# A new opening for a four-direction scan layer: order of the first loads, fillers and weight products on TensorE, earlier requests for the second step

## The chip, the cores and the metric

The kernel runs on one core of a Trainium2 chip. The metric is the device time of one execution in microseconds (us); runs of one kernel are summarised by their median. The core has TensorE (PE, matrix products into PSUM, the accumulator memory of eight banks), VectorE (DVE), ScalarE (ACT), GpSimd (POOL), SyncE (SP, which issues nearly all transfers here) and 16 DMA engines. Each engine works through its own instructions in order and waits for others on semaphores.

## What is computed

The input `x` is 4 images of 128 channels and 96x96 points, float32. Each is normalised over 32 groups of four channels, read along four directions (rows, rows reversed, columns, columns reversed), put through the same scan layer, and the four results are fused by a 1x1 product and added to `x`. Cut to what matters:

```python
def _scan1d(x, ...):                               # x: sequences of 9216 points
    t = _grouped1x1(x, in_proj_w, in_proj_b, G)    # 4 groups of 32 channels
    u, gate = (t[:, :HID], t[:, HID:])
    u = jax.nn.silu(u)
    u = lax.conv_general_dilated(u, dw_w, ...)     # depthwise, 5 taps
    s = _conv1x1(u, ssm_in_w)
    a = DMIN + (DMAX - DMIN) * jax.nn.sigmoid(_conv1x1(u, ssm_delta_w, ssm_delta_b))
    bb = jnp.tanh(_conv1x1(u, ssm_b_w, ssm_b_b))
    cc = jnp.tanh(_conv1x1(u, ssm_c_w, ssm_c_b))
    prefix = jnp.cumsum(jnp.log(a), axis=-1)
    hst = jnp.exp(prefix) * jnp.cumsum(bb * s * jnp.exp(-prefix), axis=-1)
    u = u + _conv1x1(cc * hst + ssm_d[None, :, None] * s, ssm_out_w)
    u = _grouped1x1(u * jax.nn.sigmoid(gate), mix_w, mix_b, G)
    return _conv1x1(u, out_proj_w, out_proj_b)

def _gn(v, G=32, eps=1e-5):                        # mean and variance of a group
    ...
x = x + fuse(_scan1d of the four readings of _gn(x))
```

## The kernel before

**Tiling.** A sequence is cut into `NS` = 6 steps (lines of 16 x 96 points), a step into `R` = 4 phases (every fourth point), so that a tile has `N` = 384 points. Two directions run side by side (`s` = 0, 1) in one phase of the outer loop, which has 8: two orders (columns "V", rows "H") for each of 4 images. One turn of the main loop, `pair(t)`, handles two units (both `s`) of one step and phase; there are 192 turns. The second half of each phase's steps reads the mirrored data that the first half wrote to DRAM (`kept_sil`, `kept`).

**A turn.** It convolves (`conv`, `conv_less` on TensorE for half of the channels, `taps` on ScalarE and VectorE for the other half, with the first tap, `first_tap`, on ScalarE and the following ones as `scalar_tensor_tensor` on VectorE, L667), multiplies by the four scan weights (`proj`), scans (`recurrence`), and, six turns later, makes gates and outputs (`gates_and_out`, `gating`) and accumulates them into `acc` (`accumulate`). `front(t + R)` is work for one step ahead: it multiplies `x_in` by the normalised weights (`in_proj`, 4 banks of PSUM), applies silu on ScalarE (`silu`, L511), asks for the next step's rows (`after_front`, L269) and for the store of finished silus (`keep_silu`, L491). The instructions are kept in the order written (`manual_schedule`), on every engine and on SP's queue, from `start()` on; what stands ahead of it is ordered by the scheduler.

**The statistics.** For the first image x is loaded into `acc` in eight transfers (`load_x`, L296) and VectorE makes `bn_stats` of 24 pieces as they land (L298). `stats_finish` then goes through `bn_aggr` (L188), a product with `gmean` that averages over groups (`pm`), some tiny VectorE work, a second product (`pv`), `std` by the Sqrt table on ScalarE (L211), the table of silu (L213), the scaled weights `wn` (L230) and a last group of products (`pb`) for the biases `bn`. Each averaging product is done by `product` as four products of 32 columns each (L134, the helper `mm`). For the other three images the same function is run in pieces, one in every turn with phase 2 or 3 (`stats_piece`), with the biases in two turns: the first has `gm4` times `wn` and a copy and spread on VectorE (L249, L250), the second the product with `id32` (L254). It takes the PSUM bank in `free[0]`.

**The opening.** Weights come in three transfers: `small` (42 KB), `fuse` (512 KB) and `main` (384 KB), all issued by ScalarE (L291), beside x on SP. TensorE folds the output weights: 8 products L380, copied by ScalarE to `w_of`, 8 products L387 scaled into `w_fin`, 12 products of one column for the bias `b_fin` (L395). `stay_busy` issues products that nobody reads (L302): four with 512 columns ahead of the statistics' products, one with 256 and one with 512 between them. `start()` then does step 0: four `burst(0, g)` of 8 products each, their silus, then for each g `burst(1, g)`, silus and `after_front(0, g)`. So the second step's rows are asked for by

```python
for s in range(2):
    load_front(step + 1, s, slice(64 * s + 32, 64 * s + 64), slice(g, g + 1))
if g == R - 1:
    for s in range(2):
        load_front(step + 1, s, slice(64 * s, 64 * s + 32), slice(0, R))
```

and the silus of step 0 are stored one or two at a time by the first turns, `keep_silu((1, 2, 1, 0)[t] if t < R else 0)`. Inside the first `proj`, `front(R, ...)` stands between the products of the two halves of `u`; turn 0 calls `first_tap(2)` ahead of it.

Of the kernel before, what the change touches and what calls it, by code (L numbers as in the profile page):

```python
# [67 lines left out]
def conv_preact_kernel(  # L68
# [60 lines left out]
    def bank(i):  # L129
        return psum[:, i, :]  # L130
# [45 lines left out]
    def product(o, lhsT, rhs):  # L176
        for c in range(4):
            mm(o, c, lhsT[:, 32 * c : 32 * c + 32], rhs, True, True)

    def stats_finish(b):  # L180
# [10 lines left out]
        product(pm[:, 0:1], gmean, mv[:, 0:1])  # L191
# [10 lines left out]
        for e in range(2):  # L202
            product(pv[:, e : e + 1], gmeans[:, e, :], ex)
# [8 lines left out]

# [26 lines left out]
        product(pb[:, 0:4], wn, gm4)  # L239
        if b == b0:  # L240
            for g in range(4):
                for q in range(R):
                    mm(pb[:, 4 + g : 5 + g], q, wn[0:32, 32 * g : 32 * g + 32], mean[0:32, :], True, True)
            nc.vector.tensor_sub(bn, b_in, pb[:, 0:8])
        else:
            nc.vector.tensor_sub(bn[:, 0:4], b_in[:, 0:4], pb[:, 0:4])
            spread = sp.tile([P, 4], F32, tag="spread", name=f"spread_{b}")
            shift = sp.tile([P, 1], F32, tag="shift", name=f"shift_{b}")
            nc.vector.tensor_copy(shift, pb[:, 0:1])  # L249
            nc.vector.tensor_scalar_mul(spread, gmask, shift)  # L250
            yield
            pq = bank(free[0])
            for q in range(R):
                mm(pq[:, 0:4], q, id32, spread, True, True)  # L254
            nc.vector.tensor_sub(bn[:, 4:8], b_in[:, 4:8], pq[:, 0:4])
# [33 lines left out]
    def load(src, name, pool=wp):  # L289
        t = pool.tile(list(src.shape), F32, tag=name, name=name)  # L290
        nc.scalar.dma_start(t, src)  # L291
        return t
# [6 lines left out]

    def stay_busy(n):  # L300
        if n:
            nc.tensor.matmul(  # L302
                bank(free[0] ^ 1)[:, :n], w_fin[:, 0, 0, :],
                w_fin.rearrange("p d j c -> p (d j c)")[:, :n], start=True, stop=True,
                skip_group_check=True,
            )
# [11 lines left out]
    load_x([(6, 4)])  # L318
    w_out_fuse = load(fuse, "fuse", pp)
    load_x([(10, 4)])  # L320
    w_main = load(main, "main")
    load_x([(14, 4), (18, 4), (22, 2)])
# [76 lines left out]
    for _ in range(4):  # L399
        stay_busy(512)  # L400
# [737 lines left out]
```

## Time and profile before

| what | us |
|---|---|
| median of 3 runs | 1834.1 (1832.43 to 1839.93) |
| the profiled execution: its time | 1834.1 |
| its span | 1832.3 |
| TensorE busy in the span | 1804.5 (98%) |
| ScalarE busy | 1567.5 (86%) |
| VectorE busy | 1451.7 (79%) |
| GpSimd busy | 1423.1 (78%) |
| mean granted clock of TensorE | 0.995 |

The time is 1.8 us more than the span; the difference lies outside what the profile records. Engine rows in the views have a start, a busy time, engine, line, operation, output and inputs, and a count; a bracket tells how long the engine was idle before and what ended that. One fp32 product shows as two records on TensorE (`x8` is four products), so counts there are twice those in the code. The granted clock is a share of full speed. Busy time of TensorE hides pipelining, and it hides the clock: the same product is longer when the clock is at half.

### The profile page before, as it was taken

What the parts mean: (1) busy time and instruction counts of PE and PEld (TensorE: products, weight loads), DVE (VectorE), ACT (ScalarE), POOL (GpSimd) and SP (SyncE); (2) the same over time, 40 slices, a digit from 0 to 9 for tenths busy, and PEclk for the clock granted to TensorE, in tenths of its full rate; (3) what the DMA queues carried; (4) which work ended last, traced back from release to release, by engine and by line L of the source; (5) the groups of instructions that cost most, each with busy time, mean ns of one, the idle gap of its engine ahead of it and who ended that gap; (6) DMA issues with size and microseconds to landing.
All of it is one profiled execution on the core that took longest, in us unless ns stands there. A gap on an engine that the chain in (4) does not pass through costs nothing.

```text
span 1832.3 us, 57345 instructions
## 1 busy us (share of the span) xinstructions
PE 1804.5 (98%) x24092; PEld 651.7 (36%) x24092; DVE 1451.7 (79%) x1460; ACT 1567.5 (86%) x2762; POOL 1423.1 (78%) x1469
## 2 busy tenths in 40 slices
PE   7999999999999999999999999999999999999998
PEld 4333333333333333333333333333333333333333
DVE  5888878877878888877778888877877778777886
ACT  4888888988888888888888888888888888888974
POOL 2487887778778888787877888887877788887785
PEclk8999999999999999999999999999999999999999
DMA  6755563444965566344696547443476634635434
GB/s 196 198 192 179 163 191 111 160 144 147 301 234 180 167 193 184 104 141 140 212 299 203 170 162 208 135 159 112 160 238 222 225 127 153 193 103 179 148 122 156
DMA packets 147826, 321.18 MB, mean 175 GB/s; under 512 B 14193, under 2 KB 115697, under 8 KB 147569
## 3 DMA queue, kind: packets, MB, share of 16 engines
q1 hardware_dynamic: 147136, 316.56, 53.8%
q8 instruction: 190, 3.11, 0.7%
q10 hardware_dynamic: 432, 0.96, 0.1%
q14 instruction: 68, 0.55, 0.1%
HBM read 185.21 MB, written 132.25 MB: 173 GB/s over the span
## 4 chain that ended last, share of the span: by engine, by line
PE 95%; ACT 3%; DMA 1%; DVE 1%; issue 0%; POOL 0%; SPq 0%; ACTq 0%; DVEq 0%; POOLq 0%
PE psum L134 81%; PE psum L536 8%; PE psum L530 5%; ACT sil L511 1%; ACT psum L544 1%; DMA x_in<-in_xs 0%; PE psum L302 0%; ACT u L650 0%; DMA fuse<-in_fuse 0%; ACT t L717 0%; DVE u L616 0%; ACT t L705 0%; PE psum L380 0%; ACT psum L665 0%; ACT u L648 0%
## 5 line engine op out<-in xcount | busy, mean ns | idle before, releaser
L667 DVE SCALAR_TENSOR_TENSOR psum<-sil,small,psum 128x768 f32<-128x768 f32 x576 | 589.1, 1023 | 32.3 <-ACT psum L665 6.6
L134 PE MATMUL psum<-u,w_fin 128*32 128x384 f32 x6176 | 552.6, 488 | 0.2 <-ACT t L705 0.2
L616 DVE SCALAR_TENSOR_TENSOR u<-gate,psum 128x768 f32<-128x768 f32 x376 | 349.9, 953 | 251.1 <-ACT gate L553 113.7
L134 PE MATMUL psum<-u,main 128*32 128x384 f32 x6144 | 536.0, 489 | 0.1
L786 POOL TENSOR_TENSOR acc<-ys,acc 128x384 f32<-128x384 f32 x374 | 413.6, 1127 | 36.2 <-ACT ys L767 10.4
L740 POOL TENSOR_TENSOR t<-t,t 64x384 f32<-64x384 f32 x191 | 233.4, 1222 | 156.1 <-PE psum L530 74.9
L134 PEld LDWEIGHTS psum<-u,w_fin 128*32 128x32 f32 x6176 | 189.2, 110 | 321.5 <-issue 221.0
L134 PEld LDWEIGHTS psum<-u,main 128*32 128x32 f32 x6144 | 181.6, 110 | 327.8 <-issue 199.3
L544 ACT COPY psum<-u 128x768 f32<-128x768 f32 x352 | 276.8, 799 | 22.0 <-DVE u L667 10.3
L707 POOL TENSOR_SCALAR t<-tm 64x384 f32<-64x384 f32 x191 | 176.7, 925 | 151.5 <-ACT tm L699 101.1
L134 PE MATMUL psum<-sil,band 128*32 128x384 f32 x3072 | 285.9, 488 | 3.1 <-ACT ys L769 3.1
L741 POOL TENSOR_TENSOR t<-t,t 64x384 f32<-64x384 f32 x191 | 246.4, 1290 | 15.0
L536 PE MATMUL psum<-t,main 32*128 32x384 f32 x1536 | 242.1, 515 | 3.3 <-ACT psum L544 2.6
L665 ACT ACTIVATE psum<-sil,small 128x768 f32<-128x768 f32 x192 | 174.2, 907 | 62.3 <-DVE u L616 52.3
L553 ACT ACTIVATE gate<-psum,bnorm 128x384 f32<-128x384 f32 x384 | 192.9, 582 | 28.4 <-PE psum L530 26.4
L708 POOL TENSOR_TENSOR t<-t,tm 64x384 f32<-64x384 f32 x192 | 195.1, 1016 | 15.3
L667 DVE SCALAR_TENSOR_TENSOR u<-sil,small,psum 128x768 f32<-128x768 f32 x192 | 194.9, 1015 | 8.2 <-PE psum L134 0.5
L511 ACT ACTIVATE sil<-psum,bnorm 128x385 f32<-128x385 f32 x384 | 192.1, 585 | 3.1 <-PE psum L134 0.9
L134 PE MATMUL psum<-sil,less 64*32 64x384 f32 x3072 | 168.1, 495 | 0.0
L530 PE MATMUL psum<-x_in,wn 32*128 32x384 f32 x768 | 162.1, 528 | 3.9 <-DVE shift L249 1.4
L769 ACT COPY ys<-psum 128x384 f32<-128x384 f32 x281 | 130.1, 477 | 29.1 <-PE psum L134 28.2
L134 PEld LDWEIGHTS psum<-sil,band 128*32 128x32 f32 x3072 | 89.9, 109 | 174.7 <-issue 93.9
(98 smaller groups left out, 1500.3 us busy)
## 6 DMA issues: line engine op xcount, KB each, us to landing
sil<-sil SPq DMA_DIRECT2D x128, 770.0 KB, 6.9
kept<-gate SPq DMA_DIRECT2D x80, 768.0 KB, 3.7
gate<-kept SPq DMA_DIRECT2D x76, 768.0 KB, 4.8
x_in<-in_xs SPq DMA_DIRECT2D x192, 96.2 KB, 2.5
out<-acc SPq DMA_DIRECT2D x48, 384.0 KB, 8.2
acc<-in_xr SPq DMA_DIRECT2D x38, 384.0 KB, 6.9
xs<-in_xr SPq DMA_DIRECT2D x72, 192.0 KB, 4.7
x_in<-in_xs SPq DMA_DIRECT2D x184, 48.1 KB, 3.9
```

What stands on the lines that cost most here:

```text
L134: nc.tensor.matmul(o[r, : rhs.shape[-1]], lhsT, rhs, start=start, stop=stop, skip_group_check=True)
L511: nc.scalar.activation(sils[step][:, s, j, g, :], bank(bk)[:, : N + 1], AF.Silu, bias=bn[:, 1:2] if j else bn[:, 4 + g : 5 + g],)
L530: nc.tensor.matmul(bank(to)[:, :N], stats[un["b"]][0][r, s, :], x_in[s][r, q, off : off + N], start=True, stop=True)
L536: nc.tensor.matmul(bank(SSM + 2 * s + j)[:, :N], w_so[r, bass.ts(j, P)], z[r, :], start=bi not in seeded, stop=True, skip_group_check=True)
L544: nc.scalar.copy(psum[:, SSM + 2 * s : SSM + 2 * s + 2, :N], us[bi][:, s])
L553: nc.scalar.activation(gv[:, s, j, :], bank(to[2 * s + j])[:, :N], AF.Tanh, bias=bn[:, 2 + j : 3 + j], scale=0.5,)
L616: nc.vector.scalar_tensor_tensor(v, g, 1.0, pz, ALU.add, ALU.mult)
L667: nc.vector.scalar_tensor_tensor(us[i][:, :, 1, :] if k == K - 1 else part, src, w_tap[:, k : k + 1], part, ALU.mult, ALU.add,)
L708: nc.gpsimd.tensor_mul(ta[0:64, p, :], tb[0:64, :], tm[0:64, :])
L740: engine.tensor_mul(ta[0:64, p, :], tb[64:P, :], ta[64:P, p, :])
L741: engine.tensor_add(tb[0:64, :], ta[0:64, p, :], tb[0:64, :])
L786: adder.tensor_add(part, y, part)
```

## The change

The averaging products are no longer cut in four: `product` is gone, and each is one product of 128 columns. For the later images the biases are made in one turn, as for the first, with 16 tiny products of `mean`, and the spread with `id32` is gone. `stats_piece` in turns with `ahead` set stands behind `conv_less`. `fuse` and `main` are issued by SP, behind most of x and behind all of x. VectorE's two scalings of weights go to GpSimd, behind the making of `band` and `less`. Folding is spread: three filler products with 512 columns of x, the eight `w_out` products, and then the eight `w_mix` products in four calls of `fold`, between the products of the statistics; the 12 products of one column stand behind the fourth fold and ahead of `pb`. ScalarE copies two results at a time. `stay_busy` is gone. The second step's rows are asked for by `load_rows` between the bursts, all four silu stores of step 0 at the end of `start()`, and turn 0's `first_tap(2)` is put between the second and the third silu of `front(R)`.

```diff
-    def product(o, lhsT, rhs):
-        for c in range(4):
-            mm(o, c, lhsT[:, 32 * c : 32 * c + 32], rhs, True, True)
...
-        product(pm[:, 0:1], gmean, mv[:, 0:1])
+        nc.tensor.matmul(pm[:, 0:1], gmean, mv[:, 0:1], start=True, stop=True)
...
-            product(pv[:, e : e + 1], gmeans[:, e, :], ex)
+            nc.tensor.matmul(pv[:, e : e + 1], gmeans[:, e, :], ex, start=True, stop=True)
...
             nc.scalar.activation(std, var, AF.Sqrt)
-
+            after_std()
             nc.scalar.activation(first_table, std[:, 0:1], AF.Silu)
...
-        product(pb[:, 0:4], wn, gm4)
-        if b == b0:
-            for g in range(4):
-                for q in range(R):
-                    mm(pb[:, 4 + g : 5 + g], q, wn[0:32, 32 * g : 32 * g + 32], mean[0:32, :], True, True)
-            nc.vector.tensor_sub(bn, b_in, pb[:, 0:8])
-        else:
-            nc.vector.tensor_sub(bn[:, 0:4], b_in[:, 0:4], pb[:, 0:4])
-            spread = sp.tile([P, 4], F32, tag="spread", name=f"spread_{b}")
-            shift = sp.tile([P, 1], F32, tag="shift", name=f"shift_{b}")
-            nc.vector.tensor_copy(shift, pb[:, 0:1])
-            nc.vector.tensor_scalar_mul(spread, gmask, shift)
-            yield
-            pq = bank(free[0])
+        nc.tensor.matmul(pb[:, 0:4], wn, gm4, start=True, stop=True)
+        for g in range(4):
             for q in range(R):
-                mm(pq[:, 0:4], q, id32, spread, True, True)
-            nc.vector.tensor_sub(bn[:, 4:8], b_in[:, 4:8], pq[:, 0:4])
+                mm(pb[:, 4 + g : 5 + g], q, wn[0:32, 32 * g : 32 * g + 32], mean[0:32, :], True, True)
+        nc.vector.tensor_sub(bn, b_in, pb[:, 0:8])
...
-    load_x([(6, 4)])
-    w_out_fuse = load(fuse, "fuse", pp)
-    load_x([(10, 4)])
-    w_main = load(main, "main")
-    load_x([(14, 4), (18, 4), (22, 2)])
+    load_x([(6, 4), (10, 4), (14, 4), (18, 4)])
+    w_out_fuse = load(fuse, "fuse", pp, nc.sync)
+    load_x([(22, 2)])
+    w_main = load(main, "main", wp, nc.sync)
...
+    def fold(d):
+        pt = bank((4, 5, 0, 1)[d])[:, : 2 * P]
         for j in range(2):
             nc.tensor.matmul(
+                pt[:, bass.ts(j, P)], w_mix[:, j, :], w_of[:, d, j, :], start=True, stop=True
             )
+        nc.scalar.mul(w_fin[:, d].rearrange("p j c -> p (j c)"), pt, 0.5)
+
+    with tc.manual_schedule(engines=engines):
+        for _ in range(3):
             nc.tensor.matmul(
+                bank(7), accf[:, bass.ds(10 * SC, P)], accf[:, bass.ds(10 * SC, 512)],
+                start=True, stop=True,
             )
...
+        pieces = stats_finish(b0, lambda: fold(3))
+        next(pieces)
+        fold(0)
+        next(pieces)
+        fold(1)
+        fold(2)
+        next(pieces)
...
+        for i, (lhsT, rhs) in enumerate(terms):
+            nc.tensor.matmul(
+                pf[:, 0:1], lhsT, rhs, start=(i == 0), stop=(i == len(terms) - 1)
+            )
+        for _ in pieces:
+            pass
+        nc.vector.tensor_add(b_fin, pf[:, 0:1], b_fuse)
...
-                front(R, (5, 4, 2, 3))
+                first = front_parts(R, (5, 4, 2, 3), half=True)
+                next(first)
+                next(first)
+                first_tap(2)
+                for _ in first:
+                    pass
...
         if ahead:
             accumulate(waiting.pop(0), w[1], *final)()
             free[0] = w[0]
-            stats_piece()
             if not between:
                 conv_less(i, banks)
+            stats_piece()
...
-        keep_silu((1, 2, 1, 0)[t] if t < R else 0)
...
-        pieces = stats_finish(b0)
-        for wait in (0, 256, 512, 0, 0):
-            next(pieces, None)
-            stay_busy(wait)
...
         for g in range(R):
             burst(0, g)
+        load_rows(0, slice(0, R))
         for g in range(R):
             silus(0, g)
         new_u(0)
         for g in range(R):
             burst(1, g)
+            if g in (0, R - 1):
+                load_rows(1, slice(min(g, 1), g + 1))
             silus(1, g)
-            after_front(0, g)
+            to_keep.append((0, g))
...
         taps(0, (2, 3, 4))
+        keep_silu(R)
```

## The prediction

> **What bounds the kernel now.** I read the page's engine shares first, then its slices, then TensorE's waits, the chain of the first 80 us, and the timeline and clock of the stretches the change touches.
>
> ```profile
> PE 1804.5 (98%) x24092; PEld 651.7 (36%) x24092; DVE 1451.7 (79%) x1460; ACT 1567.5 (86%) x2762; POOL 1423.1 (78%) x1469
> ...
> PE   7999999999999999999999999999999999999998
> ```
>
> TensorE sets the time; only the first and last slices are not full. Outside the opening a saved microsecond can only be one in which TensorE waits, and its waits are few:
>
> ```profile
> PE psum L380 <- DMA fuse<-in_fuse: 6.3, 1, 6.3
> PE psum L134 <- DMA x_in<-in_xs: 4.3, 2, 2.8
> ...
> PE psum L530 <- DVE shift L249: 1.4, 3, 0.5
> ...
> PE psum L530 <- DVE bnorm L255: 1.2, 3, 0.4
> ```
>
> The two waits for `x_in` stand at 34.8 (2.83 us, second step) and 61.6 (1.42 us, third step) in the timeline. The start itself is this chain of rows:
>
> ```profile
> 10.54 8.44 DVE L298 BATCH_NORM_STATS2 bn<-acc 128x6 f32<-128x384 f32 x18
> 12.21 1.84 PE L395 MATMUL psum<-small,w_of 128*128 128x1 f32 x16
> 13.92 1.41 PE L395 MATMUL psum<-small,fuse 128*128 128x1 f32 x8
> 15.19 6.68 PE L302 MATMUL psum<-w_fin 128*128 128x512 f32 x8
> 19.01 0.80 DVE L188 BATCH_NORM_AGGREGATE mv<-bn 128x2 f32<-128x144 f32 x1
> 21.80 0.24 PE L134 MATMUL psum<-mv,gmean 128*32 128x1 f32 x8
> 23.08 1.12 PE L302 MATMUL psum<-w_fin 128*128 128x512 f32 x2
> 25.59 4.84 ACT L511 ACTIVATE sil<-psum,bnorm 128x385 f32<-128x385 f32 x10 [0.45 <-PE psum L134]
> ```
>
> `mv` is ready at 19.81, but its product runs at 21.80, behind four fillers that take 1.67 us each. The clock tells why they are slow (columns: stretch, length, PE, PEld, DVE, ACT, POOL, clock, DMA share, GB/s):
>
> ```profile
> 14.80:17.80 3.00, 3.00 (x6) 1.54 (x7) 3.00 (x7) 0.26 (x1) 0.00 (x0) 0.50 1.04 322
> 17.80:21.00 3.20, 3.20 (x5) 1.35 (x4) 1.98 (x4) 0.00 (x0) 0.00 (x0) 0.50 1.07 213
> 38.40:41.60 3.20, 3.20 (x36) 0.71 (x32) 3.09 (x4) 2.38 (x5) 0.00 (x0) 0.50 0.16 36
> ```
>
> Finer stretches put the drops at 14.4 and 38.3 and the returns at 21.2 and 41.7, all whole multiples of about 3.41 us apart. The first drop follows the one-column products of L395, the second the 2.83 us wait.
>
> **The change, part by part.** Gains have a minus.
>
> 1. *Statistics sooner.* VectorE loses 0.66 + 0.15 us of weight scaling, which GpSimd does between 10.9 (its last `band`) and its next work at 42.1, free there. It also idled 1.46 and 1.57 us for x, which shared the DMA with `fuse` and `main`. Summed over stretches of 2 us, the DMA moved 4.76 MB until 14.0 and 5.55 MB until 16.0. In the new order `small`, x and `fuse` are 5.29 MB, so the last pieces arrive at 15.3 plus 0.5 (early pieces were used 0.3 to 0.75 after their bytes by the same sum). Two pieces at 0.469 and the aggregate give `mv` at 17.55 instead of 19.81. The bounds are 15.7 to 19.81: 24 pieces from 3.95 without a pause, or no gain.
>
> 2. *When TensorE can take `mv`.* The fillers need the fifth x transfer: 2.80 MB, so 9.9. Three at 1.67 last until 14.9. `fuse` lands at 14.3 + 0.5. Eight `w_out` products at 0.27 (full clock, pace of L390) to 0.43 (L383) and one fold end between 17.5 and 19.2. So the averaging product starts at 18.0, against 21.80: -3.8 (bounds -2.6 to -5.0).
>
> 3. *From there to the first silu* it was 3.79 us. Folds 1 and 2 (four products, 1.1 us) take the place of a 0.70 filler and a pause: +0.2. Between `pv` and `pb` stood 1.05 us, one filler long. Now fold 3 (0.5) and the twelve one-column products (12.21 to 15.33, 3.1 us, paced by their weight loads) stand there, and `pb`, `mean` and the bursts queue behind them: +2.5 (bounds +1.5 to +2.8). ScalarE's fourth `w_fin` scaling ahead of the silu table load (1.28 us) is hidden by this. One product of 128 columns for four of 32 costs nothing: two weight loads at 0.115 against 0.24 for the group. The second averaging product hides its 0.2 in the folds. The first silu comes at 24.5 instead of 25.6: -1.1. `x_in` must be there: the bytes ahead of it are unchanged (it landed 11.3 after its issue at 8.56), so about 20.
>
> 4. *Clock.* The fillers move from just ahead of the bursts to before the folds; what precedes the bursts is the kind of work after which the clock fell at 14.4. A burst is 0.64 us (six in 3.85 from 24.64); at half clock at most 1.28, against 0.97 for its two silus (ten in 4.84): 0.64 + 3 x 0.31 = 1.6 us. I take it at not quite even odds, +0.7 (0 to +3.2, two spells).
>
> The Trainium skill, "TensorE: Matmul & The Clock Gate", Part 1, says half clock is the default, and one window of about 3.4 us of sustained products lifts it. Here fillers ran from 15.19 and the clock rose at 21.2, 6 us later. By the rule the cold spell ends inside the four bursts and the sum stays as it is; by the row it can last two windows, and the sum loses up to 2.5 us. The same rule speaks against the change, since idle windows bring the half clock back and the filler that guarded the bursts is gone.
>
> 5. *Second step's x.* Rows of j = 0 are now asked for after the fourth burst (they landed within 4 us of asking before), and the first `front(R)` needs only one q of j = 1. The 2.83 us wait goes. What is late next is `u` of unit 0 on VectorE, done at 37.35: the second half of `proj` starts there instead of at 39.76. `first_tap(2)` waits for the same 37.35, and two silus pass ahead of it. Then VectorE's taps for the next unit end at 42.57, where `proj` started at 45.17. From the third unit on ScalarE and TensorE pace both kernels at 5.8 us a turn, and 2.4 of the 2.6 remain: -2.4 (bounds 0, if silu stores hold the rows back, to -2.6).
>
> 6. *Silu stores sooner.* Four of 0.79 MB go out from about 34 instead of 40 to 54. The DMA moved 360 GB/s around one store and 218 in the thickest stretch, so they are through between 44 and 49, before the third step's last rows are asked for. The wait at 61.6 goes: -1.4 (0 to -1.9, main products 64.55 against 62.65 by the cadence). On SP they stand ahead of the rows of `after_front` and of `xs`; VectorE takes `xs` at 50.3 before, some 48 after, with 0.8 of slack in front of TensorE: +0.3 (0 to +1.2).
>
> 7. *Later images, three times.* Two turns with 0.69 and 0.62 us around the tiny products become one with 0.23 + 0.43 + a wait of 0.47 to 0.6; the wait of 0.31 ahead of `gmean` (ScalarE's `ys`) is hidden by `conv_less`; the second averaging grows from 0.30 to 0.46. -0.2 each, -0.6 (+1.5 to -2).
>
> Sum: -1.1 + 0.7 - 2.4 - 1.4 + 0.3 - 0.6 = -4.5. The profiled execution took 1834.1 (span 1832.3 and 1.8 around it), which is also the median, so 1829.6.
>
> **Rivals.** *The start returns nothing* (1832.8): the clock is at half for the bursts (+0.9 on the value taken), and stores collide with third-step rows and `xs` (+2.3), leaving -1.3. For it: DMA shares over 1.0 from 50 to 70. Against: the stores end earlier than before, not later.
>
> *All of it arrives* (1825.6): start at -2.5 (`mv` taken at 17.6, one-column products at +1.5, clock full), -2.6, -1.9 and -1.5 in the middle, -8.5 in all. For it: TensorE has no other wait. Against: item 3 is bound by weight loads.
>
> *The clock stays low* (1836): after the bursts TensorE waits for silus and `u`, so no spell of 3.4 us is filled, and the half clock runs into the turns. There a spell costs at most 1.7 us (half of 3.41; 16 records of `main` took 2.44 us at 39.76 against 1.40 at full clock). Without the clock term the forecast is 1828.9, with 1.6 for the bursts 1830.5, so 3.6 us are left to 1834.1: it decides from the third spell after 35, a clock that is low until about 45, at 1830.5 + 3 x 1.7 = 1835.6. For it: the spell from 38.3 came after one wait. Against: cold products fill their spell by themselves, and it ended after 3.4 us.
>
> **How the numbers follow.** Forecast 50% (1827 to 1832), nothing returned 20%, all 17%, clock low 13%. A difference under 0.5%, 9.2 us, can't be told from no change by a measurement of this kernel. Faster by more (under 1824.9) takes most of the third case's lower half and a tail of item 7: 12%. Slower (over 1843.3) needs more than seven such spells: 5%. The range 1824.5 to 1834.5 leaves out the low clock and the far end of the gains.
>
> **What would show it.** `mv` near 17.5 and its product near 18; twelve one-column products right ahead of `pb`, and the first silu near 24.5; a granted clock of 0.5 or 1.0 from 21 to 28; no wait for `x_in` near 34 and 60; `proj` of unit 1 some 3 us sooner than 45.17; no VectorE wait for `xs` above 1 us near 48; one wait per image at `bnorm` instead of two. Wrong would be: any TensorE wait over 1 us between 20 and 80 that is not there now, a steady turn that is longer than 9.27 us after 80, or a third cold spell.

## The result and the profile after

The changed kernel takes 1837.84 us (median of 22 runs, 1837.3 to 1842.7); the kernel before took 1833.95 beside it (22 runs, 1830.33 to 1840.18). The ratio is 1.0022, 95% interval [1.0014, 1.003]: some 4 us slower, less than the 0.5% that the prediction took as its bound of no change, but outside its range and on the other side of zero. The profiled execution has a span of 1836.6 us against 1832.3, and the same mean clock of 0.995.

The page's first line, the engine shares, hardly differs:

```profile
PE 1803.7 (98%) x24062; PEld 651.6 (35%) x24062; DVE 1450.4 (79%) x1450; ACT 1566.6 (85%) x2753; POOL 1424.0 (78%) x1471
```

TensorE still bounds the kernel, and the loss must again lie in the opening or in its waits (what waited, for what: us in total, times, longest):

```profile
PE psum L365 <- DMA acc<-in_xr: 11.5, 1, 11.5
PE psum L134 <- DVE u L662: 4.8, 3, 2.6
...
PE psum L187 <- DVE mv L184: 1.2, 1, 1.2
PE psum L525 <- DVE bnorm L239: 1.1, 3, 0.4
```

The two waits for `x_in` are gone, and one wait for `bnorm` per image stands where there were two, as the change meant. In their place come 4.8 us for `u` (1.35 and 0.78 in the second step, 2.64 in the third), and TensorE now waits 1.2 us for `mv`, which before had to wait for TensorE. The timeline of the opening (start, busy, row):

```profile
16.55 2.05 PE L372 MATMUL psum<-fuse 128*128 128x128 f32 x16 [0.73 <-DMA fuse<-in_fuse]
18.26 1.02 DVE L282 BATCH_NORM_STATS2 bn<-acc 128x6 f32<-128x384 f32 x2 [1.07 <-DMA acc<-in_xr]
19.32 0.81 DVE L184 BATCH_NORM_AGGREGATE mv<-bn 128x2 f32<-128x144 f32 x1
20.27 0.35 PE L187 MATMUL psum<-mv,gmean 128*128 128x1 f32 x2 [1.22 <-DVE mv L184]
...
22.35 1.84 PE L388 MATMUL psum<-small,w_of 128*128 128x1 f32 x16
24.05 1.20 PE L388 MATMUL psum<-small,fuse 128*128 128x1 f32 x8
25.12 0.57 PE L235 MATMUL psum<-gm,wn 128*128 128x4 f32 x2
26.04 6.99 PE L134 MATMUL psum<-x_in,wn 32*32 32x385 f32 x96
27.67 1.06 ACT L504 ACTIVATE sil<-psum,bnorm 128x385 f32<-128x385 f32 x2 [3.22 <-PE psum L134]
```

`mv` is ready at 20.13 (19.81 before), its product runs at 20.27 (21.80), and yet the first silu comes at 27.67 (25.59). Between them stand the twelve one-column products of L388, and behind these the bursts, which take 6.99 us where the chain before had them done in about 3.9. The granted clock says why (columns: stretch, length, PE, PEld, DVE, ACT, POOL, clock, DMA share, GB/s):

```profile
4.00:6.00 2.00, 0.00 (x0) 0.00 (x0) 1.11 (x3) 0.00 (x0) 1.93 (x7) 1.00 0.98 349
6.00:8.00 2.00, 0.00 (x0) 0.00 (x0) 0.61 (x2) 0.00 (x0) 1.69 (x5) 1.00 1.00 350
...
22.00:24.00 2.00, 2.00 (x20) 2.00 (x19) 0.81 (x4) 1.68 (x4) 0.00 (x0) 1.00 0.85 228
24.00:26.00 2.00, 2.00 (x40) 1.98 (x43) 0.00 (x0) 0.44 (x2) 0.00 (x0) 0.69 0.27 77
26.00:28.00 2.00, 2.00 (x49) 0.75 (x52) 0.39 (x3) 0.33 (x1) 0.00 (x0) 0.50 0.04 8
...
34.00:36.00 2.00, 2.00 (x28) 0.38 (x20) 0.32 (x2) 1.51 (x3) 0.00 (x0) 0.75 0.47 127
```

The shares in the second and the last stretch put the fall at 24.8 and the return at 35.0: 10.2 us, three times the 3.41 us that the prediction found between changes of the clock (a window, from here on). TensorE is recorded as busy for all of 22 to 36, so "busy" did not keep the clock up. The first two stretches belong to another loss: the DMA moved 349 and 350 GB/s there, against 413 and 426 before:

```profile
6.00:8.00 2.00, 1.68 (x8) 1.68 (x9) 1.00 (x2) 0.53 (x2) 1.69 (x6) 1.00 1.04 426
```

Further on, the third step shows what became of the wait for its rows:

```profile
46.76 2.79 PE L134 MATMUL psum<-u,main 128*32 128x384 f32 x32 [0.78 <-DVE u L662]
...
55.80 1.02 DVE L421 BATCH_NORM_STATS2 bn<-xs 128x6 f32<-128x384 f32 x2 [3.97 <-DMA xs<-in_xr]
...
61.06 4.16 PE L134 MATMUL psum<-u,main 128*32 128x384 f32 x32 [2.64 <-DVE u L662]
```

VectorE waits 3.97 us for `xs`, its next taps and `u` come late, TensorE waits 2.64 us for that `u`, and its products then take 4.16 us instead of 2.79: from 62.3 to 65.7 the clock is at half once more (0.58 and 0.57 in the two stretches of 2 us from 62).

To place the loss, I followed one activation of ScalarE (`tm`, one per turn) through both profiles. Against before it comes 1.92 us later in turn 0, 1.44 and 1.57 in turns 1 and 2, 4.54 in turn 3 and 4.05 at 73 us; from there it rises to 5.43 by 1281 us, and the span ends 4.3 later. So not quite half of the loss is there at the first turn, the rest comes with `xs`, and each of the three later images adds 0.41 (near 305, 751 and 1197 us). The 1.1 us that come back at the end lie behind the last turn: the clock drops there near 1810 to 1817 us in both, for two windows before and for one in the changed kernel, where no edit was made.

### The profile page after: what moved, and what is told of

Same layout as the page of the kernel before. It is cut to its first block, busy times and chain, and to the rows that moved or that the text cites. A ratio compares the mean times of both kernels' runs of the same rounds, so it can differ in the third digit from the quotient of the medians.

```text
span 1836.6 us, 57260 instructions
## 1 busy us (share of the span) xinstructions
PE 1803.7 (98%) x24062; PEld 651.6 (35%) x24062; DVE 1450.4 (79%) x1450; ACT 1566.6 (85%) x2753; POOL 1424.0 (78%) x1471
## 4 chain that ended last, share of the span: by engine, by line
PE 95%; ACT 2%; DVE 1%; DMA 1%; issue 0%; SPq 0%; POOL 0%; DVEq 0%; POOLq 0%
PE psum L134 81%; PE psum L531 8%; PE psum L525 5%; DMA acc<-in_xr 1%; ACT sil L504 1%; DVE psum L662 0%; DMA xs<-in_xr 0%; ACT t L717 0%; SPq L280 0%; DVE u L611 0%; DVE u L662 0%; ACT t L705 0%; POOL t L707 0%; ACT tm L699 0%; PE psum L388 0%
## 5 line engine op out<-in xcount | busy, mean ns | idle before, releaser
L548 ACT ACTIVATE gate<-psum,bnorm 128x384 f32<-128x384 f32 x384 | 193.0, 582 | 28.2 <-PE psum L525 26.2
```

Of the source, the lines that this page charges most:

```text
L548: nc.scalar.activation(gv[:, s, j, :], bank(to[2 * s + j])[:, :N], AF.Tanh, bias=bn[:, 2 + j : 3 + j], scale=0.5,)
```

## The experiments

**Theory:** the twelve one-column products cost the path twice: their place between `pv` and `pb`, and the half clock that they bring upon the bursts. **Rivals:** the loads (SP alone, x first) made the start late; the early silu stores delay `xs`; the later images' 128-column averaging products cost more than they save. Three kernels undo one part of the changed one each, and `b_rows` puts one part into the kernel before.

**a_stores**: the changed kernel, the silu stores in turns 0 to 3 again.

```diff
+        keep_silu((1, 2, 1, 0)[t] if t < R else 0)
...
-        keep_silu(R)
```

> The changed kernel with the four silu stores of step 0 asked for in turns 0 to 2 again, as before. Theory (stores): the 3.97 us wait of VectorE for xs at 51.8 and the 2.64 us TensorE wait behind it come from four stores that stand ahead of xs on SP; it goes, and with it the half clock of 62.6 to 66.2. The wait for the third step's rows may come back in part (up to 1.4). So 2 to 3.5 us faster than the changed kernel, about 1.001 of before. Rival (start): the loss is made ahead of the first silu, stores cost nothing, and the time stays at 1.0022 of before.

Measured: 1837.35, ratio 1.0022 [1.0008, 1.0035], the changed kernel's own. VectorE's longest wait for `xs` fell from 3.97 to 1.5 us, but that profile started later (`mv` from 21.48 on, first silu at 28.95). So the stores delay `xs`, and in the time this can't be told from nothing.

**a_queue**: the changed kernel, `fuse` and `main` by ScalarE and between the pieces of x again.

```diff
-    load_x([(6, 4), (10, 4), (14, 4), (18, 4)])
-    w_out_fuse = load(fuse, "fuse", pp, nc.sync)
-    load_x([(22, 2)])
-    w_main = load(main, "main", wp, nc.sync)
+    load_x([(6, 4)])
+    w_out_fuse = load(fuse, "fuse", pp)
+    load_x([(10, 4)])
+    w_main = load(main, "main")
+    load_x([(14, 4), (18, 4), (22, 2)])
```

> The changed kernel with fuse and main issued by ScalarE between the parts of x again. Theory (queue): with x, fuse and main all on SP the DMA moved 350 GB/s until 8 us instead of 413 to 426, and the last x piece lies behind fuse, so x ahead of the weights brought nothing; with ScalarE's queue back mv comes at about 19.2 instead of 20.13 and the time falls by about 0.9 us. Rival (as predicted): x ahead of the weights is worth 2 us, something else made mv late, and mv comes at 21 or later, 1 us or more slower than the changed kernel.

Measured: 1835.56, 1.0015 [1.0003, 1.0028]. With the weights back *between* the pieces of x, the DMA moved 418 and 426 GB/s from 4 to 8 us, the aggregation began at 18.89 instead of 19.32, and the first silu came at 26.04 instead of 27.67. Only 0.43 of these 1.63 us are the aggregation's: in this profile the clock fell at 26.5, behind the first bursts, and not at 24.8. The time is 0.0007 better, less than the intervals tell apart; the start itself repeats in every profile: in the five kernels that load from SP alone the aggregation begins at 19.32 to 21.48, in the others, with ScalarE's two loads, at 18.86 to 19.55.

**a_fill**: the changed kernel, the one-column products moved ahead of the first averaging product, two fillers of 512 columns in their place.

```diff
         fold(0)
+        pf = bank(7)
+        for i, (lhsT, rhs) in enumerate(terms):
...
         next(pieces)
         fold(1)
         fold(2)
         next(pieces)
-        pf = bank(7)
-        for i, (lhsT, rhs) in enumerate(terms):
...
+        for _ in range(2):
+            nc.tensor.matmul(
+                bank(3), accf[:, bass.ds(10 * SC, P)], accf[:, bass.ds(10 * SC, 512)],
+                start=True, stop=True,
+            )
```

> The changed kernel with the twelve one-column products moved from between the second averaging product and the biases to ahead of the first averaging product, and two fillers of 512 columns in their place. Theory (clock): the clock fell at 24.9 because of the one-column products and stayed at half until 35.0; with fillers it stays full, the bursts take 0.64 us each instead of 1.28, and u of unit 0 comes 11.8 us after the first silu instead of 13.7. The one-column products find only 1.4 us of idle TensorE, so the start loses 1 us and the whole gains about 1 us on the changed kernel. Rival (pace of ScalarE): silus set the pace of the opening whatever the clock, and the kernel is 1 us slower than the changed one.

Measured: 1835.86, 1.0013 [1.0003, 1.0024]. The bursts did run at full clock, yet little was won. TensorE's timeline:

```profile
19.37 1.84 PE L384 MATMUL psum<-small,w_of 128*128 128x1 f32 x16
21.08 1.03 PE L384 MATMUL psum<-small,fuse 128*128 128x1 f32 x8
...
22.28 2.05 PE L358 MATMUL psum<-w_of,fuse 128*128 128x128 f32 x8
...
25.83 3.43 PE L392 MATMUL psum<-acc 128*128 128x512 f32 x4
...
29.58 3.85 PE L134 MATMUL psum<-x_in,wn 32*32 32x385 f32 x96
```

The clock fell at 22.1, behind the one-column products in their new place; the four products of folds 1 and 2 then took 2.05 us (1.14 in the changed kernel) and the two fillers 1.7 each. The products took the low clock along with them. That speaks for the theory's cause and against its remedy.

**b_rows**: the kernel before with the second step's rows asked for as in the change (`load_rows`, halves of `front(R)`, `first_tap(2)` between them), and nothing else of it.

```diff
-                front(R, (5, 4, 2, 3))
+                first = front_parts(R, (5, 4, 2, 3), half=True)
+                next(first)
+                next(first)
+                first_tap(2)
+                for _ in first:
+                    pass
...
+        load_rows(0, slice(0, R))
...
+            if g in (0, R - 1):
+                load_rows(1, slice(min(g, 1), g + 1))
             silus(1, g)
-            after_front(0, g)
+            to_keep.append((0, g))
```

> The kernel before with the second step's rows asked for between the bursts and first_tap(2) between the second and third silu of front(R), nothing else. Theory (rows): the 2.83 us wait at 34.8 goes, unit 1's proj comes 2.4 to 2.6 us sooner, and no clock drop follows at 38.3: 2.4 us faster than before, 0.9987 of it, if the third step's wait does not grow. Rival (covered): VectorE's taps set the pace of the first turns and the third step's rows come no sooner, so that most of it is given back by 64 us, and the time is within 0.5 us of before.

Measured: 1829.79, 0.9983 [0.9971, 0.9994]: faster than both kernels. In its profile the first silu comes 1.49 us sooner than before (one spell of low clock under the fillers instead of two), turn 0 comes 3.64 sooner. The 2.15 us between the two are the rows; the 1.49 are the clock's and no part of the edit.

So one part of the change gains, and the rest loses more. The next four add parts to `b_rows`, one at a time.

**r_early**: `b_rows` with the four silu stores at the end of `start()`.

```diff
-        keep_silu((1, 2, 1, 0)[t] if t < R else 0)
...
         taps(0, (2, 3, 4))
+        keep_silu(R)
```

> b_rows with the four silu stores asked for at the end of start(), nothing else: the stores' part of the change by itself. Theory (stores behind xs): xs lands late for VectorE, a wait of 1 to 4 us for xs near 48 and one of TensorE behind it; 1 to 3 us slower than b_rows (0.9983 of before), so 0.999 to 1.000 of before. Rival (as predicted): the third step's wait goes and the kernel is 0.5 us faster than b_rows. Rival (no effect, as a_stores against the changed kernel had it): equal to b_rows within 0.5 us.

Measured: 1829.02, 0.9992 [0.998, 1.0004]. In the profile turn 3 is 1.7 us late against `b_rows` (0.29 of it from the start), and all but 0.47 of it is back at 68 us. VectorE's wait for `xs` there is 2.76 us, where `b_rows` has 0.68: that is the stores. In the time they are worth nothing that can be measured, either way.

**r_later**: `b_rows` with the statistics as in the change: averaging products of 128 columns, biases in one turn, `stats_piece` behind `conv_less`.

```diff
-        product(pm[:, 0:1], gmean, mv[:, 0:1])
+        nc.tensor.matmul(pm[:, 0:1], gmean, mv[:, 0:1], start=True, stop=True)
...
-        product(pb[:, 0:4], wn, gm4)
+        nc.tensor.matmul(pb[:, 0:4], wn, gm4, start=True, stop=True)
...
-            stats_piece()
             if not between:
                 conv_less(i, banks)
+            stats_piece()
```

> b_rows with the statistics' products as in the changed kernel: averaging products of 128 columns, biases of the later images in one turn, and the pieces behind conv_less. Theory (later images): the four traces of the changed kernel's opening lose 0.9 to 1.6 us between 73 and 1282 us against before, b_rows loses nothing there; so this one is about 1.2 us slower than b_rows, three steps of 0.3 to 0.5 us near 300, 750 and 1195. Rival (as predicted): the saved turn pays, 0.6 us faster than b_rows.

Measured: 1830.73, 0.9989 [0.9977, 1.0001]. Against `b_rows` the turns are 0.73 us later at first, 1.05 at 300 us and 1.29 at 1277. There is a step of 0.41 where each image's statistics are made (near 300, 746 and 1193 us); the sum looks smaller because `b_rows` loses 0.48 of its own near 935.

**r_terms**: `b_rows` with the twelve one-column products moved from before the fillers to between `pv` and `pb`, in place of the filler there.

```diff
+            if n == 2:
+                pf = bank(0)
...
+                for i, (lhsT, rhs) in enumerate(terms):
+                    nc.tensor.matmul(
+                        pf[:, 0:1], lhsT, rhs, start=(i == 0), stop=(i == len(terms) - 1)
+                    )
```

> b_rows with the twelve one-column products between the second averaging product and the biases, in place of a filler of 512 columns. Theory (clock and place): they take 2.8 to 3.1 us where the filler took 1.1, so the bursts start 1.7 to 2 us later, and the clock falls within the following 4 us, for 1 to 2 us more; 2 to 4 us slower than b_rows, equal to before or up to 1 us above. Rival (place only): the clock stays at full through the bursts, since the fillers ran just before, and only 1.7 to 2 us are lost.

Measured: 1835.43, 1.0016 [1.0007, 1.0025]. This one edit takes back what the rows gained and as much again: 0.0033 of 1832, 6 us. But its profile had TensorE wait 4.17 us for `mv` first, and the clock was low from 20.1, ahead of the products, to 37.2. So the run shows the price, and not yet whether the wait or the products lowered the clock.

**c_best**: `b_rows` with VectorE's two scalings moved to GpSimd and three fillers instead of four.

```diff
-    nc.vector.tensor_scalar_mul(b_proj[64:P, 0:1], b_proj[64:P, 0:1], 0.5)
+    nc.gpsimd.tensor_scalar_mul(b_proj[64:P, 0:1], b_proj[64:P, 0:1], 0.5)
...
-    for _ in range(4):
+    for _ in range(3):
         stay_busy(512)
```

> b_rows with VectorE's two scalings of weights on GpSimd and three fillers of 512 columns in place of four ahead of the first averaging product. Theory: mv comes 0.66 us sooner, and TensorE is free for it at once; 0.7 us faster than b_rows, 0.998 of before. Rival: with fewer fillers the clock is at half when the bursts start, 1 us or more slower than b_rows; or x_in of step 0 is late and nothing is gained.

Measured: 1829.46, 0.9986 [0.9973, 0.9998], no gain over `b_rows`; the aggregation began at 19.07 instead of 19.16. VectorE's work was not what the statistics waited for.

**r_warm**: `r_terms` with eight fillers, so that TensorE is busy up to `mv`.

```diff
-    for _ in range(4):
+    for _ in range(8):
         stay_busy(512)
```

> r_terms with eight fillers of 512 columns in place of four, so that TensorE does not idle 4.17 us ahead of the first averaging product. Theory (one-column products lower the clock by themselves): the clock falls one spell after the twelve products begin, as at 14.4 in the kernel before, and the bursts run at half; 1 to 3 us faster than r_terms, since the twelve take 2.8 instead of 5 us, but still 2 us or more slower than b_rows. Rival (the idle stretch lowered it): the clock stays at full past the bursts, only 1.7 us of place are lost, and the time is about 5 us under r_terms, 0.9992 of before.

Measured: 1833.96, 1.0003 [0.9993, 1.0012]. The timeline and the clock by stretches:

```profile
21.18 1.95 PE L406 MATMUL psum<-small,w_of 128*128 128x1 f32 x16
22.98 1.03 PE L406 MATMUL psum<-small,fuse 128*128 128x1 f32 x8
...
24.54 6.99 PE L134 MATMUL psum<-x_in,wn 32*32 32x385 f32 x96
```

```profile
22.00:24.00 2.00, 2.00 (x24) 1.99 (x26) 0.43 (x2) 1.22 (x2) 0.00 (x0) 1.00 0.61 152
24.00:26.00 2.00, 2.00 (x65) 1.15 (x72) 0.39 (x3) 0.00 (x0) 0.00 (x0) 0.52 0.02 3
...
34.00:36.00 2.00, 2.00 (x44) 0.70 (x48) 1.08 (x2) 0.80 (x3) 0.00 (x0) 0.92 0.01 2
```

TensorE had waited 0.34 and 0.16 us since 12.8, and the clock was full until 24.1, through the one-column products. Then it fell, and came back at 34.3, 10.2 us later, with the bursts at 6.99 us, as in the changed kernel. The wait is not needed: the products bring the low clock by themselves. Fillers returned the part that `r_terms` owed to the wait (0.0013), and the products kept theirs: 0.0020 over `b_rows`, 3.7 us.

**a_noterms**: the changed kernel with a filler in place of the twelve products. It leaves out the part of the bias that they fold, so it serves only to time their absence.

```diff
-        for i, (lhsT, rhs) in enumerate(terms):
-            nc.tensor.matmul(
-                pf[:, 0:1], lhsT, rhs, start=(i == 0), stop=(i == len(terms) - 1)
-            )
+        nc.tensor.matmul(
+            bank(3), accf[:, bass.ds(10 * SC, P)], accf[:, bass.ds(10 * SC, 512)],
+            start=True, stop=True,
+        )
...
-        nc.vector.tensor_add(b_fin, pf[:, 0:1], b_fuse)
+        nc.vector.tensor_copy(b_fin, b_fuse)
```

> The changed kernel without the twelve one-column products (b_fin is then the fuse bias alone: the folded part of the bias is left out of the result), with one filler of 512 columns in their place, as before. Theory (one-column products, place and clock): 1.6 us of TensorE's time goes from the path, and the clock, which fell at 24.9 after a spell of such products, stays at full through the bursts for 2 us more: 3 to 4 us faster than the changed kernel, 1.0003 of before. Rival (place alone): the short folds lower the clock just as well, and 1.6 us are gained, 1.0013 of before. Rival (they do not matter): 1.0022.

Measured: 1833.23, 1.0003 [0.9991, 1.0014], 0.0019 less than the changed kernel, 3.5 us. Its timeline:

```profile
22.72 1.02 PE L384 MATMUL psum<-acc 128*128 128x512 f32 x2
...
24.07 3.85 PE L134 MATMUL psum<-x_in,wn 32*32 32x385 f32 x96
```

The clock is full in every stretch up to 66 us. From `pm` to the first silu it is 4.37 us (20.64 to 25.01) instead of 7.40: 1.9 by the place (0.86 from L384 to `pb`, where L388 took 2.77), 1.1 by the clock. The 3.7 us that are left above `b_rows` must lie with the other suspects.

**r_tiles**: `r_later` with the averaging products of 32 columns again.

```diff
-        nc.tensor.matmul(pm[:, 0:1], gmean, mv[:, 0:1], start=True, stop=True)
+        product(pm[:, 0:1], gmean, mv[:, 0:1])
...
-        nc.tensor.matmul(pb[:, 0:4], wn, gm4, start=True, stop=True)
+        product(pb[:, 0:4], wn, gm4)
```

> r_later with the averaging products and the gm4 product in four tiles of 32 columns again; biases of the later images still in one turn. Theory (wide products): products of 128 columns between those of 32 cost TensorE 0.3 to 0.4 us per image, and the steps of r_later's trace near 300, 746 and 1193 go; equal to b_rows within 0.5 us. Rival (merged turn): the sixteen tiny products of mean cost it, and the steps stay.

Measured: 1829.47, 0.9986 [0.9975, 0.9997]. In its profile TensorE idled 2.1 us before `mv` and the start was cold (3.79 late against `b_rows`), but from there the turns only come nearer, by 0.27 in each of the three images (to 3.46 at 384 us). So the merged turn gains 0.27 an image, and the 128-column products cost the 0.41 of `r_later` and this 0.27 besides, 0.68.

**a_undone**: `a_noterms` with ScalarE's loads, late stores and 32-column averaging products too. It puts the edits of `a_stores`, `a_queue` and `r_tiles` on top of `a_noterms`, and like it leaves out the folded part of the bias.

> The changed kernel with all but its folds, fillers and second-step requests undone: ScalarE's queue for fuse and main, the silu stores in turns 0 to 2, column tiles, no one-column products (the folded part of the bias is left out of the result) and one filler in their place. Theory: what is left of the loss was in these parts, and it comes to b_rows, 0.998 to 0.999 of before. Rival: spreading the folds over the statistics costs by itself (half clock after short folds), and it stays at before or above, 1.000 to 1.001.

Measured: 1827.23 (6 runs), 0.9967 [0.9954, 0.998]. With the four suspects gone the new opening is no worse than the old one, and its profile has no low stretch of the clock in the opening.

Open was still *what* in one-column products lowers the clock. Each loads 128 columns of weights and streams one. The sums can be had the other way round: the column as the weight, and 128 columns streamed.

```diff
-            pb[:, 0:1], lhsT, rhs, start=(i == 0), stop=(i == len(terms) - 1)
+            pb[0:1, :P], rhs, lhsT, start=(i == 0), stop=(i == len(terms) - 1)
         )
+    b_row = pp.tile([1, P], F32, name="b_row")
+    nc.scalar.copy(b_row, pb[0:1, :P])
...
+    nc.tensor.matmul(pb[:, P : P + 1], b_row, ident[0:1, 0:1], start=True, stop=True)
```

**b_swap** does this at the old place, in `b_rows`, and has five fillers there instead of four:

> b_rows with the twelve bias products turned round at their old place (ahead of the statistics' products): the one column is now the weight and the 128 columns are streamed, into one row of PSUM; the row is copied and turned back into a column by one more product. The sums are the same. Five fillers of 512 columns instead of four. In b_rows the clock fell at 15.0, straight behind the one-column products. Theory (products that load 128 columns of weights to stream a single one lower the clock, although they are recorded as busy): twelve at some 0.25 us, 12.4 to 15.5, no fall near 15; fillers at 0.85, first silu within 0.4 of 24.1, time 1829.8 +- 1 because mv at 19.0 sets the start there; fewer runs at the low mean clock of 0.994 than b_rows had (4 of 12) if those come from the same spell, the same share if not. Rival (any run of short products lowers the clock): a fall near 15 again, fillers at 1.67, first silu at 25 or later, 1831.

Measured: 1828.39, 0.9973 [0.9964, 0.9983]. The opening on TensorE and its clock:

```profile
12.11 1.91 PE L395 MATMUL psum<-w_of,small 128*1 128x128 f32 x16
13.86 1.04 PE L395 MATMUL psum<-fuse,small 128*1 128x128 f32 x8
14.82 1.98 PE L302 MATMUL psum<-w_fin 128*128 128x512 f32 x4
...
17.05 2.84 PE L302 MATMUL psum<-w_fin 128*128 128x512 f32 x6
20.50 0.24 PE L134 MATMUL psum<-mv,gmean 128*32 128x1 f32 x8 [0.61 <-DVE mv L188]
```

```profile
14.00:16.00 2.00, 2.00 (x12) 1.15 (x10) 2.00 (x6) 0.26 (x1) 0.00 (x0) 1.00 0.99 399
16.00:18.00 2.00, 2.00 (x6) 0.78 (x5) 2.00 (x6) 0.26 (x1) 0.00 (x0) 1.00 1.09 216
```

In `b_rows` the same two stretches have a clock of 0.71 and 0.50:

```profile
14.00:16.00 2.00, 2.00 (x12) 1.65 (x12) 2.00 (x5) 0.26 (x1) 0.00 (x0) 0.71 0.99 396
16.00:18.00 2.00, 2.00 (x4) 0.80 (x3) 2.00 (x5) 0.00 (x0) 0.00 (x0) 0.50 1.08 241
```

The twelve products take the same time, recorded as equally busy, and in this profile the clock does not fall. The bias is the same, so this version computes what the kernel before does and beats both. Its gain over `b_rows` is not told apart by the two intervals. The mean clocks differ: all 12 runs of `b_swap` have 0.997 or more and at most 1829.94 us, while 4 of the 12 of `b_rows` had 0.994 and 1832.98 to 1833.29, and of the five kernels with the unturned products at this place (`b_rows`, `r_early`, `r_later`, `c_best`, `r_tiles`) 20 of 59 runs had 0.995 or less.

But this does not show that the turning did it. One of these 20 was profiled, that of `r_tiles`, and there the unturned products left the clock full:

```profile
11.39 1.84 PE L382 MATMUL psum<-small,w_of 128*128 128x1 f32 x16
13.10 1.03 PE L382 MATMUL psum<-small,fuse 128*128 128x1 f32 x8
13.99 3.68 PE L289 MATMUL psum<-w_fin 128*128 128x512 f32 x8
19.81 0.28 PE L134 MATMUL psum<-mv,gmean 128*32 128x1 f32 x8 [2.14 <-DVE mv L188]
```

```profile
14.00:16.00 2.00, 2.00 (x7) 1.03 (x7) 2.00 (x6) 0.26 (x1) 0.00 (x0) 1.00 0.98 396
```

Its four fillers ran at full clock and ended 2.14 us ahead of `mv`; the clock fell at 19.7, in that wait, and stayed low for four windows. The fifth filler of `b_swap` leaves a wait of only 0.61, which can explain its even clock as well. And the borders of the windows, counted back in steps of 3.4133 us (a third of the 10.240 in the traces) from each profile's first change of the clock, cut the twelve products in two in `r_tiles` (at 12.9) and in `b_swap` (at 13.8), with folds or fillers in the rest of both windows; in `b_rows` the border at 14.8 left 2.4 of their 2.8 us in one window. So `b_swap` is a better kernel, and it does not separate the turning from the filler and from where the borders fell.

**a_swap** does it at the new place, in the changed kernel:

> The changed kernel with the same twelve products turned round at their place between pv and pb, and the row turned back into a column behind pb. Theory (the one-column products lower the clock for the bursts): twelve at some 0.25 us take about 3.1 us where they took 2.8, plus 0.2 for the last product; no fall of the clock at 24.8; bursts in about 3.9 us instead of 6.99; together some 2.5 us less than the changed kernel, 1835.3. Rival (the clock falls for the waits of 1.07 and 1.22 us ahead of the statistics' product, or for any short products): the clock falls between 22 and 28 as before and the time is 1838 to 1839.

Measured: 1836.18, 1.0012 [1.0, 1.0024], 0.0010 less than the changed kernel, which the intervals do not tell apart. Its timeline and clock:

```profile
21.06 0.35 PE L187 MATMUL psum<-mv,gmean 128*128 128x1 f32 x2 [1.38 <-DVE mv L184]
...
23.43 3.33 PE L388 MATMUL psum<-w_of,small 128*1 128x128 f32 x16
26.60 1.04 PE L388 MATMUL psum<-fuse,small 128*1 128x128 f32 x8
```

```profile
22.00:24.00 2.00, 2.00 (x15) 1.55 (x14) 1.01 (x6) 1.41 (x5) 0.00 (x0) 0.74 0.81 216
24.00:26.00 2.00, 2.00 (x12) 1.18 (x10) 0.00 (x0) 1.43 (x2) 0.00 (x0) 0.50 0.28 81
26.00:28.00 2.00, 2.00 (x28) 1.38 (x29) 0.00 (x0) 0.25 (x1) 0.00 (x0) 0.91 0.00 0
28.00:30.00 2.00, 2.00 (x60) 1.01 (x65) 0.49 (x3) 0.00 (x0) 0.00 (x0) 1.00 0.04 8
```

Half of each side was right. The clock did fall, at 23.0, ahead of the twelve products and behind the 1.38 us wait for `mv` and the short products of the statistics, as the rival had it. But streaming brought it back at 26.4, after 3.4 us, and the bursts ran at full clock (0.81 and 3.93 us around the last product), where one-column products had left it low for 10.2. The window that brought it back, 23.0 to 26.4, held 0.5 us of folds and otherwise turned products. In `r_terms` a whole window at half clock, 23.5 to 26.9, held unturned ones (L406, 21.71 to 26.92), recorded as just as busy, and the clock stayed down:

```profile
24.00:26.00 2.00, 2.00 (x11) 2.00 (x11) 0.00 (x0) 0.00 (x0) 0.00 (x0) 0.50 0.00 0
```

This pair, one profile each, shows what `b_swap` can't: which way round the operands stand decides. In time it brought the opening little here: turn 0 is 0.58 us later than in the changed kernel (the aggregation began 0.79 later), and the 1.7 us that the turns are ahead from 73 us on were all gained in the third step, where no second low stretch followed.

## Why the prediction was wrong

It forecast 4.5 us less; the profiled span shows 4.3 more. By its own terms:

| term | forecast | the changed kernel's profile |
|---|---|---|
| first silu against before (items 1 to 3) | -1.1 | +2.1 |
| from there to turn 2: clock and rows (items 4, 5) | -1.7 | -0.5 |
| stores, third step, `xs`, up to 73 us (item 6) | -1.1 | +2.5 |
| later images to the end (item 7) | -0.6 | +0.2 (+1.4 at 1281 us) |

**Items 1 and 2 fell.** `mv` was to be ready at 17.55 and was at 20.13. The step that failed is the sum over bytes, in two ways. It took the rate of the kernel before for another way of asking: from SP alone the DMA moved 349 and 350 GB/s where it had moved 413 and 426, and by the same sum the 5.29 MB had moved at 16.0 instead of 15.3. That is 0.7 of the 2.6 us. And it let the last pieces of x land when the bytes asked for up to them had moved. VectorE got them at 18.26, when some 5.9 MB had: `main`, `fuse` and the last pieces became late together, `fuse` 11.5 us after its issue instead of 5.0, `main` 14.1 instead of 7.0. Whether the queue or the order did it stays open, since `a_queue` undoes both. The bound of "no gain", 19.81, was no bound; a loss should have been allowed. (The other bound is mis-added: 24 pieces from 3.95 and the aggregate give 16.0, not 15.7.) The averaging product at 20.27 still beat 21.80, because it no longer stood behind cold fillers, but by 1.5 and not by the 2.6 to 5.0 forecast.

**Item 3 was right in the mechanism.** The weight loads pace the twelve products, and they stand in front of `pb`: forecast 3.1 us, measured 2.77 at a clock that was still full for most of them, with the weight loads (PEld) busy for all of 22 to 24. From `pm` to the first silu it took 7.40 instead of 6.5; the clock's 1.1 (`a_noterms`) cover the 0.9 more.

**Item 4 named the mechanism and mis-sized it.** The forecast was +0.7 at "not quite even odds" and two spells at most. The spell came in the changed kernel, in `r_terms` and in `r_warm`; it lasts three windows, five in `r_terms` and two in `a_queue`. At the first silu it cost 1.1 us (the clock's part in `a_noterms`), and more behind: `r_warm` is 3.7 us above `b_rows` for a place that costs 1.7 (from `ex` to `pb` 3.0 against 1.35). The rival that the clock stays low, 13%, was nearest, though by its third spell it reckoned from 35 on; in the event the first three ran together from 24.8, with the bursts inside. Its "against", that cold products fill their spell by themselves, is what failed: bursts of 32x32 tiles, recorded as busy all the time, did not. (At full clock the same bursts kept it: before, the window from 24.7 to 28.1 held nothing else, and the clock stayed up.)

The Trainium skill, "TensorE: Matmul & The Clock Gate", Part 1, on which the forecast leaned for one spell, lets one busy window of about 3.4 us lift the half clock. `a_swap` agrees (23.0 to 26.4, under turned products); the changed kernel does not (28.2 to 31.6 held bursts alone, and the clock stayed at half until 35.0).

**Item 5 was right.** The wait for `x_in` near 34 is gone, and the rows alone gave 2.15 us in the profile (forecast 2.4) and 0.9983 in the time.

**Item 6 was right about the waits and too low about the price.** No wait for `x_in` near 60 is left. The delay of `xs`, bounded at 1.2, was 3.97 us on VectorE and 2.64 on TensorE, and the second low clock from 62.3 came with it, so in the changed kernel the third step lost 2.5 us instead of gaining 1.1. Where no second low stretch followed, the delay was mostly caught up (`r_early` 1.7 late against `b_rows`, then 0.47; `a_queue` 1.85 late against before, then 0.0 at 73 us). That the second spell made it permanent is argued from this one profile, not shown: with the stores late again the time did not move (`a_stores`).

**Item 7 had the wrong sign.** Its merged turn was right: with 32-column products it gains 0.27 an image in the profile (`r_tiles`), where 0.2 was forecast with the wide ones. The step that failed is the price of the wide products, 0.16 us in item 7 and nothing in item 3: between other 32-column products they cost 0.68 an image (`r_later` against `r_tiles`), so that the change loses 0.41. In the time the two runs are not told apart (0.9989 and 0.9986).

How the 4 us of loss divide in the time: the twelve products 3.5 (`a_noterms`), and all four suspects together 10 (`a_undone`, 1.0022 to 0.9967), against a gain by the rows of about 3 (`b_rows`). Loads, stores and averaging products are 6.6 of these 10 together (`a_noterms` to `a_undone`, 1.0003 to 0.9967); singly each stayed within the intervals (`a_queue` 0.0007, `a_stores` 0, `r_later` 0.0006 over `b_rows`), so in the time how they divide it stays open. The profiles of `a_noterms` and `a_undone` place the 5.1 us between their spans: 0.74 at the first turn, where the loads act, 0.56 in the third step, where the stores act, 2.1 at the three images, and 2.1 behind the last turn, where the half clock lasts two windows and one; 0.3 goes the other way. The last part is not shown to belong to any edit.

## What to carry to other kernels

A filler is not replaced by just any work: products that load 128 columns of weights and stream one are recorded as busy and can still lose the clock when they fill most of a window (`r_warm`; in `r_tiles`, cut in two by a border, they did not), so keep them away from the path, or turn them round so that the many columns are streamed. Ask for the DMA rate again when loads change their queue or order, since the old rate belongs to the old arrangement. And a part of a change is worth running alone: here one part gained 3 us, and the others took back 7.

## What the runs showed of the hardware that was not expected

- Low-clock stretches came in whole windows: 3.4 us (`b_rows`, 14.8 to 18.2; `a_swap`, 23.0 to 26.4), 6.8 (`a_queue`, 26.5 to 33.4), 10.2 (the changed kernel; `r_warm`, 24.1 to 34.3), 13.7 (`r_tiles`, 19.7 to 33.4) and 17.1 (`r_terms`, 20.1 to 37.2). Behind the bursts it was a window with 2.0 to 2.7 us of `band` products (128x32 tiles) that brought the clock back, in all six profiles whose bursts ended at half clock; windows of bursts alone did not. Why is not shown.
- Each of the 16 profiles has another half-clock stretch between 1803 and 1821 us, of one window (seven) or two (nine). From the last `tm` to the end of the span it is 35.9 to 36.0 us with one and 36.6 to 38.5 with two, so two spans can differ by up to 2.6 us for this alone.
- The same loads moved 277 to 353 GB/s between 4 and 8 us in the five profiles that issue all large ones from SP, and 407 to 436 in the eleven where ScalarE issues two of them. The Trainium skill, "DMA: Bandwidth & Descriptors", section "Issuing engines are not separate DMA queues", says that issuing from several engines saves only the time to initiate; these rates differ. The order of the transfers differs too, so the queue alone is not shown to be the cause.
- The start varies from profile to profile: with identical loads from SP the aggregation began at 19.32, 19.68, 19.89, 20.11 and 21.48.
